# Attention over mirrored positions: context rows at p, 255-p, 256+p and 511-p, the reversed ones moved by index

## The chip, the cores and the metric

One Trainium2 chip, and of it one core. The metric is the time of one execution of the whole program on the device, in microseconds; lower is better. The program has five instruction streams of its own: TensorE (PE, with its weight loads apart as PEld), VectorE (DVE), ScalarE (ACT), GpSimd (POOL) and SyncE (SP). Each works through its instructions in the order written and waits for others by semaphores. SP and POOL also issue transfers between the memories. Those issued on POOL can add to what lies at their target (`accum_op`) and can take their row numbers from a tile (`indirect_dma_start`).

## The reference

`x` and `ctx` are 32 x 512 x 512 (batch, position, feature), float32. Two stages follow one another:

```python
q   = layernorm(x) * scale(norm of the row) * wave(position)
Q, K, V = q @ Wq.T + bq, (gain * ctx) @ Wk.T + bk, (gain * ctx) @ Wv.T + bv
Qf, Kf, Vf = (fft over the 512 positions)
QKV = hamilton(hamilton(Qf * filt, Kf * filt), Vf * filt)   # quaternion products in four blocks of 128 features
x   = x + ifft(QKV).real
t   = layernorm(layernorm(x)) * gamma + beta                # 16384 tokens
e   = argmax(t @ gate.T);  slot = rank among the tokens of expert e, kept while below 1024
x   = x + layernorm(x) + weight * (gelu(t @ wi[e]) @ wo[e]) # 8 experts, 512 -> 2048 -> 512
```

Since the inputs are real, half of the frequencies do. The transform is a matrix product with tables of cosines and sines.

## The kernel before

**Attention and routing** (`attention_and_routing`) runs over the 32 batch rows. For each row the 512 positions lie in four tiles of 128 (`TC = 4`). Position n and n+256 are folded: their sum gives the even frequencies, their difference the odd ones. The sum is folded once more for the even ones. `load` brings a row in on SP; `fold` (L422, L424) on DVE and `fold_sum` (L430, an accumulating transfer on POOL) fold both the context (`cs`) and the scaled input (`qs`). `forward` (L452, L457) then makes, for each of four chunks of 128 features, 256 odd columns out of two tiles of 128 positions and two times 128 even columns out of one tile each, all in one PSUM tile of the pool `ps_f` (two buffers); ACT copies it out (L465).

`project` (L483) multiplies frequencies by Wk, Wq and Wv, in two halves of frequencies (c = 0 even, 1 odd), each into one tile of `ps_p` (two buffers). ACT takes the upper half out (`halves`, L499), DVE makes the blocks from it (`block`, L506). For c = 0 the Nyquist frequency lies in a row of its own, which goes through memory and back (`nyquist_lanes`: L525 and L533 on SP, L538 and the spreads L545 to L547 on POOL). `matrix_product` (L586 to L599) makes the two quaternion products on DVE, `components` (L610 to L618) lays the result down as `y`.

The way back is in two parts. `inverse_even` (L646) has four matmuls that contract over 64 frequencies each; `second` (L652) and `even` (L656) combine them. `inverse_odd` (L661) has two matmuls for each of two position tiles, and `odd` (L672) adds and subtracts and sums at the same time. `means` (L683) makes the mean of it, and `add_input` (L701, POOL) adds the input `x` from memory, 1024 KB. One and two rows later come the second normalisation (`square` L695, `norms`, `token` L759, `result` L767 on ACT), two stores on SP (L772: the tokens to `tokbuf`, the result to `out`), the tokens' transposes (L781), the gate (`logits`, `shares`, `add_shares`), `choose`, `ranks` (L861, L862: rank by a triangular matrix) and `place`; `scatter` (L887, POOL) writes token number and weight of each token at its expert's slot into `meta`, four index transfers a row.

`stats` (L342, L346 on ACT) reads a second copy of `x` ahead of time for its mean and variance; `factors` makes the scale of several rows at once out of it with some 60 small DVE instructions, spread in steps.

**The order.** Everything in this stage is put on a written time line: `at(time, function)`, `steps(time, step, generator)`, with `ROW = 61.0` as the written length of a row. `plan.run()` issues in order of these times and `in_order` fixes that order on each engine. The written times order instructions; they hold nothing back on the chip.

**Experts** (`experts`): for each of 8 experts 2 x 512 slots are gathered from `tokbuf` by index (L1220), transposed (L1238) and sent through two matrix products (L1109), made of seven instead of eight block products (sums on DVE), and scaled and added to `out` by index (L1259). `ms` (L1197, SP) reads `meta` back once before.

Of the kernel before, what the change touches and what calls it, by code (L numbers as in the profile page):

```python
# [11 lines left out]
F32 = mybir.dt.float32  # L12
# [5 lines left out]
P = 128  # L18
# [11 lines left out]
def _constants():  # L30
# [11 lines left out]

    sig = lambda v: 1.0 / (1.0 + np.exp(-v))
# [8 lines left out]
    fwd, fwdq, inv = [], [], []  # L52
    for c in range(2):
# [3 lines left out]
        e = np.exp(-2j * np.pi / S * ((np.arange(h)[:, None] * k[None, :]) % S))  # L57
        herm = np.zeros(P, np.complex128)
# [6 lines left out]
        f, q, i = pack(e), pack(e * herm), pack(e)  # L65
        if c == 0:
            alt = 1.0 - 2.0 * (n % 2)
            f[:, P] = i[:, P] = alt
            q[:, P] = alt * filt3[h].real
        fwd.append(f)  # L70
        fwdq.append(q)
        inv.append(i.T * (0.5 * gain * gain / S))
    def parts(even, odd):
        even = even[0:P].reshape(P, 2, 2, P // 2).transpose(0, 2, 1, 3).reshape(P, 1, 2 * P)
        return np.concatenate([even, odd.reshape(2, P, 2 * P).transpose(1, 0, 2)], axis=1)

    fwd, fwdq = (parts(*a) for a in (fwd, fwdq))
    inv = [a.reshape(2, P, h).transpose(1, 0, 2) for a in inv]
    inv = np.concatenate([inv[0][:, :, 0:P], inv[1]], axis=2)
# [17 lines left out]
def tile_xattn_ffn(ctx: ExitStack, tc: tile.TileContext, a: dict, gain: float):  # L97
# [10 lines left out]
    meta = [dram.tile([n_slot, 2], I32, name=f"meta{t}") for t in range(TC)]  # L108
# [103 lines left out]
def attention_and_routing(tc, a, gain, ident, gamma, beta, tokbuf, meta):  # L212
    nc = tc.nc
    x_in, ctx_in = a["x"], a["ctx"]
    H = TC // 2
# [8 lines left out]
    ROW = 61.0  # L224
    base = [0.0] + [53.1 + ROW * b for b in range(B + 2)]
    end = base[B]
    marks = {}
    with ExitStack() as es:
# [25 lines left out]
        rows = lambda ap: ap.rearrange("(c p) n -> p c n", p=P)  # L254
        w = [{} for _ in range(B)]
# [4 lines left out]
        fwd = fwdp.tile([P, 1 + H, 2 * P], F32, name="fwd")  # L260
        fwdq = fwdp.tile([P, 1 + H, 2 * P], F32, name="fwdq")
        inv = wp.tile([P, 2, P + HS], F32, name="inv")
# [7 lines left out]
        tri = wp.tile([P, P], F32, name="tri")  # L270
        iota8 = wp.tile([P, TC, E], F32, name="iota8")
        iota8m = wp.tile([P, TC, E], F32, name="iota8m")
        itok = wp.tile([P, TC], F32, name="itok")
        empty = wp.tile([P, E * CAP // P, 2], I32, name="empty")
# [34 lines left out]
        def small_tables():  # L309
            nc.vector.memset(gate, 0.0)  # L310
            nc.vector.memset(ones, 1.0)
            nc.vector.memset(empty[:, :, 0], int(UNFILLED))
            nc.vector.memset(empty[:, :, 1], 0)

            nc.gpsimd.affine_select(
                tri, ones, pattern=[[1, P]], compare_op=ALU.is_gt, fill=0.0, base=0, channel_multiplier=-1
            )
            for t, pattern, by in ((iota8, [[0, TC], [1, E]], 0), (itok, [[P, TC]], 1)):
                nc.gpsimd.iota(
                    t, pattern=pattern, base=0, channel_multiplier=by, allow_small_or_imprecise_dtypes=True  # L320
                )
# [33 lines left out]
        def first_stats(t):  # L355

            if "mx" not in w[0]:
                w[0]["mx"] = sm.tile([P, TC, 2], F32, tag="mv", name="mx")
            mv = w[0]["mx"]
            st = sm.tile([P, 6], F32, tag="bnst", name=f"bx_{t}")  # L360
            nc.vector.bn_stats(st, w[0]["xs"][:, t, :])
            nc.vector.bn_aggr(mv[:, t, :], st)
            if t == TC - 1:
                nc.vector.tensor_scalar(nmean[:, 0, :], mv[:, :, 0], -1.0, None, ALU.mult)
                nc.vector.tensor_scalar(vsum[:, 0, :], mv[:, :, 1], float(D), None, ALU.mult)
# [45 lines left out]
        def load(b, n, src):  # L411
            w[b][n] = inp.tile([P, TC, D], F32, tag=n, name=f"{n}_{b}")
            nc.sync.dma_start(w[b][n], tok_rows(src[b]))

        def fold(b, n, tag, i):


            if i == 0:
                w[b][tag] = foldp.tile([P, 2, H, D], F32, tag=tag, name=f"{tag}_{b}")
            src, to = w[b][n], w[b][tag]  # L420
            if i == 0:
                tt(to[:, 1], src[:, 0:H, :], src[:, H:TC, :], ALU.subtract)  # L422
            else:
                tt(to[:, 0, i - 1, :], src[:, 0, :], src[:, 1, :], (ALU.add, ALU.subtract)[i - 1])  # L424

        def fold_sum(b, n):

            src = w[b][n]
            upper = src[:, H:TC, :] if n == "x" else tok_rows(ctx_in[b])[:, H:TC, :]
            nc.gpsimd.dma_start(src[:, 0:H, :], upper, accum_op=ALU.add)  # L430

        def fold_sum_now(b, n):
            src = w[b][n]
            tt(src[:, 0:H, :], src[:, 0:H, :], src[:, H:TC, :], ALU.add)
# [9 lines left out]
        def forward(b, src, table, tag, t):  # L444

            def mm(dc):
# [3 lines left out]
                even = ps[:, 0:HS].rearrange("p (r q f) -> p q r f", r=2, q=2)  # L450
                for i in range(H):
                    nc.tensor.matmul(  # L452
                        ps[:, HS:], w[b][src][:, 1, i, dc * P : (dc + 1) * P], table[:, 1 + i, :],
                        start=(i == 0), stop=(i == H - 1),
                    )
# [7 lines left out]
            for dc in range(DC):  # L463
                at(t + 1.31 * dc, mm, dc)
                at(t + 1.31 * (dc + 1) + 0.05, lambda dc=dc: nc.scalar.copy(w[b][tag][:, dc, :], w[b]["ps", tag, dc]))  # L465
# [880 lines left out]
```

## Time and profile before

| | |
|---|---|
| time, three runs | 3691.69 us median (3690.15 to 3692.68) |
| the profiled execution | 3692.56 us, its span 3690.9 us |
| mean granted TensorE clock | 0.986 |
| first matmul of row 0, of row 1, of row 31 | 10.44, 75.27, 1943.31 us |
| a plain row, from its first `ps_cf` matmul to the next row's | 61.32 us |
| first gather of the experts, first transposes of theirs | 2078.57, 2086.26 us |
| from the experts' first product to the end | 2094.01 to 3690.9 us |

A line of a group gives the source line, engine, operation, tiles and shapes, the number of instructions, their busy time, the mean time of one, and the idle time of the engine before them with what ended it. A line of the timeline gives start and length in us, and in brackets the idle time before it. `LDWEIGHTS` are weight loads, `DMA_DIRECT2D` and `DMA_INDIRECT` the issue of a transfer and not its movement. Names stand without buffer numbers.

### The profile page before, as it was taken

What the parts mean: (1) busy time and instruction counts of PE and PEld (TensorE: products, weight loads), DVE (VectorE), ACT (ScalarE), POOL (GpSimd) and SP (SyncE); (2) the same over time, 40 slices, a digit from 0 to 9 for tenths busy, and PEclk for the clock granted to TensorE, in tenths of its full rate; (3) what the DMA queues carried; (4) which work ended last, traced back from release to release, by engine and by line L of the source; (5) the groups of instructions that cost most, each with busy time, mean ns of one, the idle gap of its engine ahead of it and who ended that gap; (6) DMA issues with size and microseconds to landing.
All of it is one profiled execution on the core that took longest, in us unless ns stands there. A gap on an engine that the chain in (4) does not pass through costs nothing. (4 is left out here: it accounts for less than half of the span.)

```text
span 3690.9 us, 39046 instructions
## 1 busy us (share of the span) xinstructions
PE 3576.5 (97%) x14208; PEld 2461.0 (67%) x14208; DVE 2548.0 (69%) x4768; ACT 1342.5 (36%) x2563; POOL 626.9 (17%) x626
## 2 busy tenths in 40 slices
PE   8899999999999999999998599999999999999998
PEld 4455455545555545555554488888888888888887
DVE  7898989989898989898988444344444444443532
ACT  5556565645454434444443311211222222111211
POOL 2122122223231212121211111011111111111100
PEclk9999999999999999999999799999999999999999
DMA  5454455454544343434333402031313121121200
GB/s 182 126 137 130 134 138 137 132 132 110 131 112 107 94 101 101 109 99 110 98 83 95 125 23 89 12 100 35 103 35 92 46 66 54 46 69 41 86 1 1
DMA packets 256585, 334.06 MB, mean 91 GB/s; under 512 B 69572, under 2 KB 136132, under 8 KB 256391
## 3 DMA queue, kind: packets, MB, share of 16 engines
q1 hardware_dynamic: 205970, 239.92, 19.4%
q0 software_dynamic: 50128, 91.24, 14.0%
q8 instruction: 112, 1.84, 0.2%
q14 instruction: 81, 0.66, 0.1%
q10 hardware_dynamic: 294, 0.40, 0.0%
HBM read 239.63 MB, written 84.55 MB: 88 GB/s over the span
## 5 line engine op out<-in xcount | busy, mean ns | idle before, releaser
L1109 PE MATMUL r_o<-wo,h 128*128 128x256 f32 x3584 | 781.2, 379 | 0.0
L1109 PE MATMUL r<-xt,wi 128*128 128x256 f32 x3584 | 777.9, 379 | 0.8 <-DVE u L1124 0.8
L1109 PEld LDWEIGHTS r<-xt,wi 128*128 128x128 f32 x3584 | 681.7, 190 | 93.7 <-DVE u L1124 1.1
L1109 PEld LDWEIGHTS r_o<-wo,h 128*128 128x128 f32 x3584 | 677.5, 190 | 90.3
L483 PE MATMUL pp_v<-wv,cf 128*128 128x512 f32 x1024 | 459.5, 597 | 2.4 <-DVE u L396 2.3
L483 PE MATMUL pp_k<-wk,cf 128*128 128x512 f32 x1024 | 458.8, 596 | 0.0
L483 PE MATMUL pp_q<-wq,qf 128*128 128x512 f32 x1024 | 454.7, 592 | 0.0
L483 PEld LDWEIGHTS pp_k<-wk,cf 128*128 128x128 f32 x1024 | 190.1, 191 | 242.1 <-issue 236.3
L483 PEld LDWEIGHTS pp_q<-wq,qf 128*128 128x128 f32 x1024 | 192.2, 190 | 230.1 <-issue 223.6
L1285 ACT ACTIVATE h<-h 128x512 f32<-128x512 f32 x256 | 160.2, 631 | 472.3 <-DVE h L1117 471.2
L483 PEld LDWEIGHTS pp_v<-wv,cf 128*128 128x128 f32 x1024 | 188.1, 191 | 206.7 <-issue 203.5
L887 POOL DMA_INDIRECT meta<-row,slot x128 | 226.1, 1766 | 447.4 <-DVE slot L877 391.8
L1259 POOL DMA_INDIRECT out<-o,tid x64 | 107.1, 1674 | 916.0 <-ACT o L1256 802.5
L586 DVE TENSOR_TENSOR pa<-blk 128x1024 f32<-128x1024 f32 (+1 forms) x128 | 156.8, 1225 | 111.0 <-POOL blk L547 99.9
L1256 ACT ACTIVATE o<-u_o,wgt 128x256 f32<-128x256 f32 x96 | 43.7, 502 | 385.7 <-DVE u_o L1117 385.7
L1124 DVE TENSOR_TENSOR u_o<-r_o,p_o 128x512 f32<-128x512 f32 x16 | 11.1, 693 | 239.6 <-PE r_o L1109 239.6
L1117 DVE TENSOR_TENSOR h<-r,u 128x512 f32<-128x512 f32 x192 | 129.0, 687 | 68.7 <-PE r L1109 68.7
L1220 POOL DMA_INDIRECT g<-tokbuf,gid x64 | 79.5, 1242 | 514.5 <-PE ept L1238 490.8
L589 DVE TENSOR_TENSOR pa<-pa,pb 128x1024 f32<-128x1024 f32 (+1 forms) x128 | 157.1, 1227 | 2.0
L661 PE MATMUL odd<-y,inv 128*128 128x512 f32 x256 | 126.1, 629 | 31.9 <-DVE r L656 20.2
L586 DVE TENSOR_TENSOR pb<-blk 128x1024 f32<-128x1024 f32 (+1 forms) x128 | 156.7, 1224 | 0.0
L591 DVE TENSOR_TENSOR pa<-pa,pb 128x1024 f32<-128x1024 f32 (+1 forms) x128 | 156.4, 1222 | 0.0
(197 smaller groups left out, 4813.9 us busy)
## 6 DMA issues: line engine op xcount, KB each, us to landing
ctx<-in_ctx SPq DMA_DIRECT2D x32, 1024.0 KB
xs<-in_x SPq DMA_DIRECT2D x32, 1024.0 KB
x<-in_x SPq DMA_DIRECT2D x32, 1024.0 KB
r<-in_x POOLq DMA_DIRECT2D x32, 1024.0 KB
tokbuf<-tok SPq DMA_DIRECT2D x32, 1024.0 KB
out<-r SPq DMA_DIRECT2D x32, 1024.0 KB
wi<-in_wi SPq DMA_DIRECT2D x64, 512.0 KB
wo<-in_wo SPq DMA_DIRECT2D x32, 1024.0 KB
```

The source lines that it names most:

```text
L483: nc.tensor.matmul(w[b][key][:, ri, :], w[b][f][:, dc, lo : lo + P], wt[n][:, dc, :], start=(dc == 0), stop=(dc == DC - 1),)
L586: tt(out, _bc(left, full), right, ALU.mult)
L589: tt(pa[:, :, 0], pa[:, :, 0], pb[:, :, 1], ALU.subtract)
L591: tt(pa[:, :, 1], pa[:, :, 1], pb[:, :, 0], ALU.add)
L661: nc.tensor.matmul(ps, inv[:, ri, (1 + t) * P : (2 + t) * P], w[b]["y"][:, 1, ri, :], start=(ri == 0), stop=(ri == 1))
L887: nc.gpsimd.indirect_dma_start(out=meta[t], out_offset=bass.IndirectOffsetOnAxis(ap=w[b]["slot"][:, t : t + 1], axis=0), in_=w[b]["row"][: ...
L1109: nc.tensor.matmul(to[:, m, :], lhs(a, m, i), rhs(b, i), start=(i == 0), stop=(i == k - 1))
L1117: tt(c[i], x, y, ALU.add)
L1220: nc.gpsimd.indirect_dma_start(out=t, out_offset=None, in_=tokbuf, in_offset=bass.IndirectOffsetOnAxis(ap=gid[:, e, c : c + 1], axis=0), b ...
L1256: nc.scalar.activation(o[:, d * N : (d + 1) * N], c[2 * h + d][:, m, :], AF.Copy, scale=wgt[:, e, col : col + 1])
L1259: nc.gpsimd.indirect_dma_start(out=a["out"], out_offset=bass.IndirectOffsetOnAxis(ap=tid[:, e, col : col + 1], axis=0), in_=o, in_offset=None,
L1285: [lambda o=o: nc.scalar.activation(o, o, AF.Gelu) for o in out],
```

## The change

The context's positions are laid down in four mirrored places: partition p holds p, 255-p, 256+p and 511-p. The two forward places come with one plain load (`onward`), the two reversed ones by index transfers of 128 rows each (`behind`, with the row numbers in `back`). Sums and differences over these four places separate cosines from sines as well as even from odd frequencies. So the context's forward transform has four matmuls of 128 columns for each chunk, and the odd frequencies need one tile of places where they had two. The way back is four matmuls of 512 columns over 128 frequencies, cosines and sines apart, in the order (even, odd); `sines`, `part`, `upper` and `lower` put the four places together. The input path keeps its positions and its table.

With it move: the context's sums and half of the input's go to accumulating transfers on POOL (`add_ctx`, `add_x`, `add_x_quarters`, `lower`), negated copies to ACT (`minus_ctx`, `minus_x`, `signed_x`), the sums for the mean to ACT (`sum_up`), which now runs after the input is added. Input and result meet the mirrored layout by index: `add_input` and the store to `out` are one plain and two index transfers each. `meta` has three words an entry, `ranks` two triangular matrices, and the written times are new, with `ROW = 57.5`, other times for nearly every step, and other groups of rows for `factors`. The core of it:

```diff
@@ attention_and_routing
-    ROW = 61.0
-    base = [0.0] + [53.1 + ROW * b for b in range(B + 2)]
+    ROW = 57.5
+    base = [0.0] + [50.4 + ROW * b for b in range(B + 2)]
+        def onward(ap):
+            return ap.rearrange("(h w p) d -> w p h d", h=H, p=P)[0]
+
+        def behind(b, ap, tiles, store=False, add=False):
+            for h, t in enumerate(tiles):
+                at_row = bass.IndirectOffsetOnAxis(ap=back[:, b, h : h + 1], axis=0)
+                ins = nc.gpsimd.indirect_dma_start(
+                    out=ap if store else t,
+                    out_offset=at_row if store else None,
+                    in_=t if store else ap,
+                    in_offset=None if store else at_row,
+                    bounds_check=n_tok - 1,
+                    oob_is_err=False,
+                    **({"compute_op": ALU.add} if add else {}),
+                )
+            return ins
...
-                tt(to[:, 1], src[:, 0:H, :], src[:, H:TC, :], ALU.subtract)
-                tt(to[:, 0, i - 1, :], src[:, 0, :], src[:, 1, :], (ALU.add, ALU.subtract)[i - 1])
-            nc.gpsimd.dma_start(src[:, 0:H, :], upper, accum_op=ALU.add)
...
+        def load_ctx(b):
+            w[b]["ctx"] = c = inp.tile([P, 2, H, D], F32, tag="ctx", name=f"ctx_{b}")
+            nc.sync.dma_start(c[:, 0], onward(ctx_in[b]))
+            behind(b, flat_rows(ctx_in), [c[:, 1, h] for h in range(H)])
+        def minus_ctx(b):
+            c = w[b]["ctx"][:, 1]
+            nc.scalar.activation(c, c, AF.Copy, scale=-1.0)
+        def add_ctx(b, i):
+            c = w[b]["ctx"]
+            nc.gpsimd.dma_start(c[:, i], onward(ctx_in[b]) if i else c[:, 1], accum_op=ALU.add)
+        def fold_ctx(b, i):
...
+            tt(w[b]["cs"][:, i], c[:, :, 0], c[:, :, 1], (ALU.add, ALU.subtract)[i])
+        def minus_x(b):
+            new_qs(b)
+            nc.scalar.activation(w[b]["qs"][:, 1], w[b]["x"][:, H:TC, :], AF.Copy, scale=-1.0)
+        def add_x(b, i):
+            to = w[b]["x"][:, H:TC, :] if i else w[b]["qs"][:, 1]
+            nc.gpsimd.dma_start(to, w[b]["x"][:, 0:H, :], accum_op=ALU.add)
+        def signed_x(b, i):
+            nc.scalar.activation(w[b]["qs"][:, 0, i, :], w[b]["x"][:, 3, :], AF.Copy, scale=(1.0, -1.0)[i])
+        def add_x_quarters(b):
+            nc.gpsimd.dma_start(
+                w[b]["qs"][:, 0], w[b]["x"][:, 2:3, :].to_broadcast([P, H, D]), accum_op=ALU.add
+            )
...
+            def context(ps, dc):
+                for i, to in ((0, 0), (2, 3), (1, 1), (3, 2)):
+                    nc.tensor.matmul(
+                        ps[:, to * P : (to + 1) * P], w[b]["cs"][:, i // 2, i % 2, dc * P : (dc + 1) * P], fwd[:, i, :],
+                        start=True, stop=True,
+                    )
...
+        def inverse(b, c):
+            for ri in range(2):
+                w[b]["ps", c, ri] = ps = ps_f.tile([P, D], F32, tag="psf", name=f"back_{b}_{c}_{ri}")
+                nc.tensor.matmul(ps, inv[:, 2 * c + ri, :], w[b]["y"][:, c, ri, :], start=True, stop=True)
+        def sines(b, c):
...
+            nc.scalar.copy(si, w[b]["ps", c, 1])
+        def part(b, c, i):
+            co, si = w[b]["ps", c, 0], w[b]["si", c]
+            if c == 0:
+                tt(w[b]["r"][:, i, :], co, si, (ALU.add, ALU.subtract)[i])
+            else:
+                w[b]["odd"] = w[b]["y"][:, 0]
+                tt(w[b]["odd"][:, i, :], *((si, co) if i else (co, si)), (ALU.add, ALU.subtract)[i])
+        def upper(b):
+            tt(w[b]["r"][:, H:TC, :], w[b]["r"][:, 0:H, :], w[b]["odd"], ALU.subtract)
+        def lower(b, now=False):
...
+                nc.gpsimd.dma_start(r, w[b]["odd"], accum_op=ALU.add)
+        def add_input(b, way):
+            r = w[b]["r"]
+            if way:
+                behind(b, flat_rows(x_in), [r[:, 2 * h + 1] for h in range(H)], add=True)
+            else:
+                nc.gpsimd.dma_start(r[:, 0::2, :], onward(x_in[b]), accum_op=ALU.add)
+        def sum_up(b, t):
+            r = w[b]["r"][:, t, :]
+            nc.scalar.activation(r, r, AF.Identity, accum_out=sums(b)[:, t : t + 1])
...
         def store(b, to, n):
-            marks[n, b] = nc.sync.dma_start(tok_rows(to[b * S : (b + 1) * S, :]), w[b][n])
+            rows = to[b * S : (b + 1) * S, :]
+            if n == "tok":
+                marks[n, b] = nc.sync.dma_start(tok_rows(rows), w[b][n])
+            else:
+                nc.sync.dma_start(onward(rows), w[b][n][:, 0::2, :])
+                marks[n, b] = behind(b, to, [w[b][n][:, 2 * h + 1] for h in range(H)], store=True)
...
-            nc.tensor.matmul(flat(rk), tri, flat(w[b]["hot"]), start=True, stop=False)
-            nc.tensor.matmul(flat(rk), ones, flat(before[b][:, 0:TC, :]), start=False, stop=True)
+            for way in range(2):
+                to = rk[:, way::2, :]
+                nc.tensor.matmul(to, tri[way], w[b]["hot"][:, way::2, :], start=True, stop=False)
+                nc.tensor.matmul(to, ones, before[b][:, way:TC:2, :], start=False, stop=True)
...
             forward(b, "cf", o, 0.875)
```

## The prediction

> **What bounds the kernel now.** I read the page first, then the stretches of equal rows, TensorE's timeline over one row, and the waits. (A row is one of the 32 batch rows; between two rows' first ps_cf matmuls.)
>
> ```profile
> PE 3576.5 (97%) x14208; PEld 2461.0 (67%) x14208; DVE 2548.0 (69%) x4768; ACT 1342.5 (36%) x2563; POOL 626.9 (17%) x626
> 895.25:956.57 61.32, 61.32 (x213) 33.19 (x212) 55.24 (x105) 32.18 (x64) 16.21 (x16) 1.00 0.47 121
> 1636.72:1698.04 61.32, 61.32 (x214) 33.20 (x213) 55.38 (x105) 26.90 (x47) 11.91 (x16) 1.00 0.42 104
> 1326.68:1391.01 64.33, 61.59 (x214) 33.11 (x213) 58.25 (x134) 26.81 (x47) 12.21 (x16) 1.00 0.39 99
> PE odd L661 <- DVE r L656: 20.2, 10, 6.9
> DVE pa L586 <- POOL blk L547: 99.9, 28, 5.4
> ```
>
> The first line is the page's busy time of each engine. The stretches give length, then busy time of PE, PEld, DVE, ACT and POOL with instruction counts, then granted clock, DMA share and GB/s; the last two lines are waits: who waited for whom, us in total, times, longest. A plain row takes 61.32 us and PE fills all of it, at full clock: PE sets the row. DVE has only 6 us to spare. In 1326.68:1391.01 the code adds 29 small DVE instructions (`factors`), DVE grows by 2.9 us and the row by 3.0: PE then waits for `even` (L656) to free a PSUM tile. This is the only PE wait of weight between rows 1 and 31.
>
> ```profile
> 1201.85 1.03 PE L452 MATMUL ps_cf<-fwd,cs 128*128 128x256 f32 x4
> 1202.71 0.61 PE L457 MATMUL ps_cf<-fwd,cs 128*128 128x128 f32 x4
> 1203.15 1.03 PE L452 MATMUL ps_cf<-fwd,cs 128*128 128x256 f32 x4
> 1222.62 0.60 PE L781 MATMUL pt<-ident,tok 128*128 128x128 f32 x4
> 1223.06 3.60 PE L483 MATMUL pp_q<-wq,qf 128*128 128x512 f32 x8
> 1234.77 1.99 PE L646 MATMUL even<-y,inv 64*128 64x512 f32 x8
> 1236.69 1.06 PE L798 MATMUL lp<-tokT,gate 128*32 128x512 f32 x8
> 1242.03 4.02 PE L661 MATMUL odd<-y,inv 128*128 128x512 f32 x8
> 1245.89 3.60 PE L483 MATMUL pp_k<-wk,cf 128*128 128x512 f32 x8
> ```
>
> Distances of starts are the real prices (ends overlap): one context chunk 1.31 us, of which four 128-column records take 0.44; four 128x128 transposes 0.44, so 0.11 a record; eight 512-column records 3.44; the even way back 1.92, the odd 3.86.
>
> **PE, part by part.** (1) Context forward: four chunks of sixteen records that were half 256 wide become four of eight records, 128 wide: 8 x 0.11 = 0.875 us each. Saved 4 x (1.31 - 0.875) = 1.74 us. (A matmul leaves two records here: four of 256 columns are two matmuls.) (2) Way back: 1.92 + 3.86 = 5.78 becomes four full matmuls, 3.44. Saved 2.34. The Trainium skill, "TensorEngine Tiling (Array Packing)", section "When to Use Tiling", speaks against giving up the even half: contracting over 64 rows allows two row tiles at once, which would be worth a factor of two. By it the old even part should take 1.72 and odd 3.44, and the saving is 5.16 - 3.44 = 1.72. The trace has 1.92 and 3.86 (0.42 of the latter waits for L656), so I take 2.34. (3) `ranks`: four small matmuls for two; L861 and L862 took 0.36 together, so +0.34. Net 3.74: row 57.6. A context chunk now fills a PSUM tile every 0.875 us, with two tiles; ACT's copy takes 0.59 (L465) and begins some 0.2 after the matmul, so a tile comes free 1.67 after its chunk's start, needed at 1.75. For this I add 0.15 (0 to 0.8). Row 57.75, 3.57 less; over rows 1 to 31 110.7 us, and 1.7 in row 0: 112.4.
>
> **DVE and its waits.** Removed per row at the timeline's cadence: L422 and L424 for both inputs 4.7, L656 1.3, L672 2.7, L683 and L847 0.2. Added: two 1024-wide context folds 2.3, four `part` 2.7 (L656's price), `upper` 1.1. Net -2.8: 52.6 of 57.75, a margin as thin as before. But both ways back now free their PSUM before the next row's forward, and `factors` is spread over more rows. From 75.27 to 1943.31 the rows lost 1868.0 - 30 x 61.32 = 28.4 us; I expect 17 back (6 of the rest in rows 1 to 3, 5 in rows 4 to 15; bounds 0 and 28). With L656's stall gone, what is late next is `block` (L506): it frees the projections' two PSUM tiles. q0's must be free before k1 starts, 8 us after DVE's turn by the written times, so DVE may lag by several us before PE stops.
>
> **ACT.** Added: `minus_ctx`, `minus_x` (1024 wide; no such row: between 0.96, twice the 0.48 cadence of a 512-wide copy, and 1.6, twice L439's 0.81; I take 1.1 each), `signed_x` 1.0, `sum_up` 2.5 (L342's cadence), one more copy 0.5, `means` 0.2; a gain is excluded, it is all new work. 26.9 + 6.4 = 33.3, and 5.3 (32.2 - 26.9) for each row's statistics, two in rows 1 to 14: 43.9 of 57.75. PE covers it; if that cover goes, it is the PSUM copies that come late.
>
> **POOL and DMA.** Here nearly all new work lies. Per row six index transfers (two each for the context load, the input added, the result's store), five direct transfers in place of three, and all in one queue with `offset`, the spreads and the four scatters.
>
> ```profile
> 832.68 5.89 POOL L887 DMA_INDIRECT meta<-row,slot  x1 [12.69 <-DVE slot L877]
> 838.87 2.01 POOL L887 DMA_INDIRECT meta<-row,slot  x1 [0.30 <-issue]
> 1261.77 1.28 POOL L887 DMA_INDIRECT meta<-row,slot  x1 [12.22 <-DVE slot L877]
> 1263.36 1.43 POOL L887 DMA_INDIRECT meta<-row,slot  x1 [0.30 <-issue]
>   POOL out L1259: 105.3, 37
> ```
>
> Ten index transfers at L887's mean 1.77 + 0.30 are 20.7; `add_x` twice, `add_ctx` twice, the quarters, `lower`, half of the input at 0.93 to 1.36 (L430, L701) 7.3; `blk<-bias` 1.7; spreads 1.9: 31.6. Waits: the input waits for `lower` to land (an L430 transfer landed within 7.4 us, issue 1222.29 to its reader at 1229.69), the first store for SP's half of the same store (5), the second for the first, since both write `out` (105.3 / 37 = 2.85). Behind these stand the scatters and the second `add_ctx`, for which `fold_ctx` on DVE waits. Sum 47, 10 below the row: no PE time. By the page "SBUF — State Buffer", section "Who interferes with whom", a DVE instruction with two SBUF inputs contends with a GpSimd one that reads SBUF, and one blocks the other fully. Then the six would each wait out a run of L586 and L589, as the 5.89 seems to: 6 x 4.6 = 28 more, a round of 75, over the row. But at 1261.77 the issue lay under four L586 in a row and took 1.28. I take the row's mean. SP issues as many transfers as before, context and result half as large, so its queue costs nothing more. DMA share: about 2.1 MB more are accumulated per row (four of 512 KB). The page's q0 moved 91.24 MB in 14.0% of the span, 5.7 us a MB: 12 us more on the 25.7 of a plain row (0.42 x 61.3), 0.65 of 57.75, and 0.7 with statistics: busy, not full; a transfer that must land within 8 us of its issue still does.
>
> **Start and tail.** The first context rows come by index after an iota: PE starts 1 to 3 us later, and row 0 waits less for statistics (DVE waited 8.6 for ACT there). The other moves of row 0 (weight v turned on ACT, row 1's statistics on DVE) go with these: zero, between -4 and +4. In the tail row 30's two indexed stores stand on POOL ahead of row 31's scatters, and wait for SP's half. That was issued at 2061.58, the scatters began at 2063.45. Now 0.4 + 5 + 1.6 + 2.85 + 1.6 come first: scatters near 2073, and the first gather (2078.57) 9.5 late. SP's `ms` loads (12 bytes an entry for 8) are behind row 31's store as well, but the `wo` load, which was issued just ahead of them at 2065.29, now stands earlier: -2.5, for `ms` took 7 us from its issue at 2069.76 to its reader at 2076.82. Net +7, between 0 and 15.
>
> **Sum.** Against the profiled execution's own 3692.56 (span 3690.9 and 1.7 around it): 3692.56 - 112.4 - 17 + 7 = 3570.2. It lies 0.9 above the median shown, so 3569. The experts, 1597 us from 2094 on, keep their code.
>
> **Rivals.** A: ACT late in rows 1 to 14. 43.9 busy in strict order, with waits for landings (`sum_up`) among the PSUM copies. For: the density. Against: ACT was at 36 to 39 of 61 in such rows before with hardly a PE wait. If they run at 59.8: 14 x 2 = 28, so 3597. B: 128-wide matmuls limited by their weight load: a LDWEIGHTS lasts 190 ns. If each record took that, the context costs 6.1, not 3.5: 32 x 2.6 = 83, so 3652. Against: the transposes' 0.11. C: POOL's round partly blocked. With 5.89 for the first of two series and waits of 19 in place of 15: 31.6 + 9.2 + 19 = 60, rows of 60: 30 x 2.25 = 67, so 3636. D, slower: the same queue, its place the store pair. If under a DMA share of 0.65 every landing waited for (`lower`, SP's half, the first store) takes the 7 us that L430's took at most, and three series begin with a 5.89, a round is 31.6 + 21 + 3 x 4.6 = 66. The change loses from a round of about 61.6 on; at 66 it is 30 x (66 - 57.75) = 248 on 3569, so 3817. For: each POOL wait holds all that is behind it. Against: 10 us of room by the mean. E: nothing moves, since PE waits for DVE as before (61.3 rows).
>
> **Chances.** Forecast 0.60 (its own range 3540 to 3590), A 0.13, B 0.04, C 0.10, D 0.11, E 0.02. Faster 0.87, same 0.02, slower 0.11; 0.2%, 7 us, is what a measurement of this kernel can tell from no change. Low end: all 28 us of waits gone, rows at 57.6, tail 0: 3540. High: takes in A, B and half of C: 3650.
>
> **What would show it.** Right: rows of 57.6 to 58.2 between first ps_cf matmuls with PE full, chunks 0.875 apart, four back matmuls in 3.44, POOL near 30 busy a row, first gather later after row 31 than 135 us. Wrong: a PE wait named ACT cf/qf or DVE blk in plain rows; DVE `cs` waiting for a DMA in every row; POOL without idle time.

## The result and the profile after

The changed kernel takes 3643.94 us (median of 4 runs, 3643.74 to 3645.2) beside 3691.44 before: ratio 0.9872, interval 0.9855 to 0.9889. It is faster, by 47.5 us, where the prediction had 122. The first matmuls of the rows cut the profiled executions into three pieces:

| us | before | after | moved | predicted |
|---|---|---|---|---|
| start to row 1's first matmul | 75.27 | 67.31 | -7.96 | -1.7 |
| rows 1 to 30 | 1868.04 | 1828.85 | -39.2 | -124.1 |
| row 31's first matmul to the end | 1747.6 | 1745.9 | -1.7 | +3.4 |
| span | 3690.9 | 3642.1 | -48.8 | -122.4 |

The last column is the prediction's sum by the same pieces: 3.57 on TensorE for each row, 17 of waits, +7 in the tail. Start and tail came out a few microseconds better; all that is missing, 85 us, is missing in rows 1 to 30. From the page, the stretches of two rows (length, then busy PE, PEld, DVE, ACT, POOL, granted clock, DMA share, GB/s), and the waits of PE and DVE:

```profile
PE 3486.9 (96%) x14080; PEld 2414.2 (66%) x14080; DVE 2467.8 (68%) x4494; ACT 1524.3 (42%) x2981; POOL 1024.4 (28%) x946
1657.00:1716.77 59.77, 58.75 (x209) 31.67 (x208) 52.51 (x94) 32.98 (x61) 28.36 (x25) 1.00 0.63 142
867.84:929.14 61.30, 58.74 (x209) 31.68 (x208) 54.19 (x111) 38.28 (x78) 27.78 (x27) 1.00 0.64 146
PE pp_v L573 <- DVE before L947: 24.6, 20, 2.2
PE pp_v L573 <- DVE blk L596: 18.6, 21, 3.6
DVE pa L676 <- DMA blk<-bias: 136.9, 44, 5.4
DVE pa L676 <- POOL blk L637: 53.9, 17, 5.4
```

A plain row fell from 61.32 to between 59.4 and 60.5. DVE, ACT, POOL and the DMA share are busy much as forecast (52.6, 33.3, 31.6 and 0.65). New are the two waits of PE in the list: PE, which waited for nothing in a plain row before, now waits for DVE to free `ps_p`. The prediction had named a wait for `blk` in plain rows as a sign of being wrong. And DVE, with 52.5 us of work in a row of 59.8, itself waits, above all for `blk<-bias`: the `offset` transfer, which adds the bias to one row of `blk` ahead of each quaternion product for c = 0. Where that wait arises is read from the timelines of POOL and DVE over one row (start, length, in brackets the idle time before):

```profile
1692.84 1.22 POOL L512 DMA_DIRECT2D qs<-x  x1 [1.85 <-ACT qs L508]
1695.27 0.90 POOL L759 DMA_DIRECT2D r<-y  x1 [1.21 <-DVE den L967]
1700.52 0.81 POOL L628 DMA_DIRECT2D blk<-bias  x1 [4.35 <-DVE slot L982]
1702.08 0.69 DVE L689 TENSOR_TENSOR o<-pa 128x516 f32<-128x516 f32 x1
1706.81 1.23 DVE L676 TENSOR_TENSOR pa<-o,blk 128x1032 f32<-128x1032 f32 x1 [4.04 <-DMA blk<-bias]
```

In before, the same pair stood so:

```profile
1241.85 0.83 POOL L538 DMA_DIRECT2D blk<-bias  x1 [7.34 <-DVE blk L506]
1242.60 1.41 DVE L656 TENSOR_TENSOR r<-even,r 128x512 f32<-128x512 f32 x2
1245.14 0.68 DVE L672 SCALAR_TENSOR_TENSOR r<-r,odd 128x512 f32<-128x512 f32 x1
1248.81 1.23 DVE L586 TENSOR_TENSOR pa<-o,blk 128x1032 f32<-128x1032 f32 x1
```

Before, the second product began 6.96 us after the offset's issue, and DVE filled the time with the way back (L656, L672) and `choose`. After, that work is elsewhere: DVE is ready 2.3 us after the issue and starts 6.3 us after it, once the 4 KB have landed. Ahead of them in POOL's queue stand two new accumulating transfers of 512 KB, the quarters (`add_x_quarters`, L512) and `lower` (L759). On SP's queue two transfers were issued shortly before, `load_x` (L446, 1024 KB) and the plain half of a store to `out`:

```profile
1698.38 1.60 SPq L446 DMA_DIRECT2D x<-in_x  x1
1700.09 0.50 SPq L875 DMA_DIRECT2D out<-r  x1
```

### The profile page after: what moved, and what is told of

Its sections match the earlier page's. It is cut to its first block, busy times and chain, and to the rows that moved or that the text cites. A ratio compares the mean times of both kernels' runs of the same rounds, so it can differ in the third digit from the quotient of the medians.

```text
span 3642.1 us, 39892 instructions
## 1 busy us (share of the span) xinstructions
PE 3486.9 (96%) x14080; PEld 2414.2 (66%) x14080; DVE 2467.8 (68%) x4494; ACT 1524.3 (42%) x2981; POOL 1024.4 (28%) x946
## 3 DMA queue, kind: packets, MB, share of 16 engines
q0 software_dynamic: 83088, 189.84, 26.1%
q1 hardware_dynamic: 189586, 206.50, 18.1%
## 5 line engine op out<-in xcount | busy, mean ns | idle before, releaser
L573 PE MATMUL pp_v<-wv,cf 128*128 128x512 f32 x1024 | 470.0, 603 | 56.5 <-DVE before L947 24.6
L1385 POOL DMA_INDIRECT out<-o,ids x64 | 106.8, 1668 | 912.5 <-ACT o L1382 803.1
L1346 POOL DMA_INDIRECT g<-tokbuf,ids x64 | 80.4, 1256 | 508.9 <-PE ept L1364 490.5
L676 DVE TENSOR_TENSOR pa<-o,blk 128x1032 f32<-128x1032 f32 (+1 forms) x124 | 152.1, 1227 | 103.8 <-DMA blk<-bias 60.5
L676 DVE TENSOR_TENSOR pa<-blk 128x1024 f32<-128x1024 f32 (+1 forms) x128 | 156.3, 1221 | 87.1 <-DMA blk<-bias 75.5
L1382 ACT ACTIVATE o<-u_o,wgt 128x256 f32<-128x256 f32 x96 | 43.5, 500 | 385.8 <-DVE u_o L1241 385.8
L992 POOL DMA_INDIRECT meta<-entry,slot x128 | 167.3, 1307 | 57.1 <-issue 36.9
L896 ACT ACTIVATE tokT<-pt,beta,gamma 128x512 f32<-128x512 f32 x124 | 96.1, 777 | 177.2 <-PE pt L885 168.7
L271 POOL DMA_INDIRECT out<-r,back x64 | 124.8, 1950 | 126.6 <-ACT cf L555 50.9
L679 DVE TENSOR_TENSOR pa<-pa,pb 128x1024 f32<-128x1024 f32 (+1 forms) x128 | 157.1, 1227 | 2.9
```

Source lines behind the costliest of these rows:

```text
L271: ins = nc.gpsimd.indirect_dma_start(out=ap if store else t, out_offset=at_row if store else None, in_=t if store else ap, in_offset=None ...
L573: nc.tensor.matmul(w[b][key][:, ri, :], w[b][f][:, dc, lo : lo + P], wt[n][:, dc, :], start=(dc == 0), stop=(dc == DC - 1),)
L676: tt(out, _bc(left, full), right, ALU.mult)
L679: tt(pa[:, :, 0], pa[:, :, 0], pb[:, :, 1], ALU.subtract)
L896: nc.scalar.activation(to, ps, AF.Identity, bias=o, scale=g)
L992: nc.gpsimd.indirect_dma_start(out=meta[t], out_offset=bass.IndirectOffsetOnAxis(ap=w[b]["slot"][:, t : t + 1], axis=0), in_=entry[:, b, t ...
```

## The experiments

Theory 1: the transfers ahead of the offset in POOL's queue make it land late, DVE has nothing left to cover that, and PE waits for DVE. Rivals: it is the offset's own latency; POOL's round with its index transfers; ACT; or the load on the DMA engines, from whichever queue. All edits are against the changed kernel. "Rows" is the sum of rows 1 to 30, and 30 rows at TensorE's own pace, shown below to be 58.27, would be 1748.1. "Waits" is DVE's for `blk<-bias` in the whole run.

| kernel | median us | ratio to before | rows | waits (times) |
|---|---|---|---|---|
| the changed kernel | 3643.94 | 0.9872 [0.9855, 0.9889] | 1828.9 | 136.9 (44) |
| e1_no_bias | 3606.95 | 0.9772 [0.9756, 0.9788] | 1788.9 | none |
| e2_ring_order | 3649.82 | 0.9888 [0.9872, 0.9905] | 1832.9 | 66.5 (20) |
| e3_way_back_between | 3615.41 | 0.9791 [0.9774, 0.9807] | 1805.3 | 44.1 (12) |
| e4_lower_on_dve | 3601.93 | 0.9761 [0.9744, 0.9777] | 1782.0 | 10.1 (6) |
| e5_lower_alone | 3624.66 | 0.9810 [0.9793, 0.9826] | 1805.1 | 68.6 (30) |
| e6_quarters_alone | 3592.53 | 0.9724 [0.9707, 0.9740] | 1774.8 | 13.7 (9) |
| e7_floor | 3596.33 | 0.9732 [0.9716, 0.9748] | 1781.5 | none |
| e8_plain_not_indexed | 3625.18 | 0.9808 [0.9792, 0.9825] | 1820.4 | 103.2 (33) |
| e9_half_quarters | 3631.43 | 0.9823 [0.9808, 0.9839] | 1808.4 | 99.5 (33) |
| e10_same_bytes_other_queue | 3599.26 | 0.9736 [0.9721, 0.9751] | 1784.7 | 14.4 (8) |
| e11_quarters_and_tail | 3600.11 | 0.9743 [0.9729, 0.9756] | 1779.0 | 18.2 (8) |
| e12_row29_store_first | 3584.17 | 0.9705 [0.9688, 0.9721] | 1779.5 | 21.6 (11) |

**The offset taken away (e1).**

```diff
 def nyquist_lanes(b, lo, hi, t, t_blk):
-            at(t_blk, offset)
```

> Leaves out the accumulating transfer of the biases (offset, L628), so bq, bk and bv are missing from the result; nothing else is changed. Theory 1: DVE sets the row of the changed kernel (52.5 us of work and 6 to 7 of waits), and most of the waits are for the landing of blk<-bias (136.9 us in 44 waits). Without it the rows go from about 60.3 to about 58.8, where TensorE alone sets them: 1.5 x 30 = 45 us, so about 3599. Theory 2: the waits only fill time that DVE would lose elsewhere, behind the spreads of the Nyquist lanes (L637): rows stay at 60 and the time within 8 us of 3644.

37 us less. Most rows from 16 on are 58.27 or 58.28 long. PE is then busy throughout, so this is TensorE's own length of a row:

```profile
1740.91:1799.18 58.27, 58.27 (x209) 31.83 (x208) 52.69 (x95) 32.96 (x61) 23.53 (x24) 1.00 0.67 145
```

About half of what rows 1 to 30 hold over TensorE's pace (80.7 us) goes with the offset, nearly all of it in the later rows: rows 14 to 30 fall from 1028.3 to 993.7 us, rows 3 to 13 only from 667.1 to 666.8. In those DVE waits for the spread (L637) instead, as the run's theory 2 had it: 127.6 us in the whole run, 53.9 before. The spread needs `nyi`, which comes back over SP's queue:

```profile
671.48 0.18 POOL L635 COPY blk<-nyi 128x4 f32<-128x4 f32 x1 [11.80 <-DMA nyi<-nyid]
```

Whether the offset is late by its own latency or by other transfers, this run can't say.

**Order in the queue, first attempt (e2).** The quarters and `lower` both go behind the second offset, and `load_x`, which overwrites what the quarters read, later with them:

```diff
-            at(t1 + 4.6, lower, b)
+            at(t1 + (11.0 if 0 < b < B - 2 else 4.6), lower, b)
-                    at(o + tf + 1.3, add_x_quarters, b + 1)
+                    at(o + (39.1 if 1 < b < B - 1 else tf + 1.3), add_x_quarters, b + 1)
-                at(o + tl, load_x, b + 2)
+                at(o + (46.0 if b > 1 else tl), load_x, b + 2)
```

> Only the order on POOL changes in rows 2 to 29: add_x_quarters and lower (512 KB each) are issued after the second offset and its spread instead of before; load_x stands 5.5 us later on SP. Theory 1 with the ring as the cause: the 4 KB of the second bias wait behind 1.5 MB of accumulating transfers; issued ahead of two thirds of them they land in about 2 us as before instead of 6.3, DVE's second wait (about 4 us a row) falls to 0 or 1, rows at about 59: 28 x 1.3 = 36 us, so about 3608. Theory 1 with a fixed latency of such a transfer as the cause (nothing between the two products for DVE to do): no change within 8 us. Theory 2: no change.

No gain, and yet the second offset was cured. POOL's and DVE's timelines:

```profile
1700.90 0.81 POOL L628 DMA_DIRECT2D blk<-bias  x1 [11.55 <-DVE slot L982]
1703.26 1.23 DVE L676 TENSOR_TENSOR pa<-o,blk 128x1032 f32<-128x1032 f32 x1
1703.39 2.02 POOL L759 DMA_DIRECT2D r<-y  x1
1711.60 1.21 POOL L766 DMA_DIRECT2D r<-in_x  x1 [6.19 <-DMA r<-y]
1678.03 1.22 DVE L480 TENSOR_TENSOR cs<-ctx 128x1024 f32<-128x1024 f32 x1 [3.83 <-issue]
```

The offset is used 2.4 us after its issue, with no wait shown. But the input may only be added once `lower` has landed, and `lower` now comes just ahead of it: POOL stands still for 6.2 us, 173.5 in 27 rows, and all behind it in the queue comes later by as much. `add_ctx` is among it, and `fold_ctx` (L480) on DVE has 82.5 us of idle time before it in 25 places, where the changed kernel has none of weight. One wait had been traded for another. This is the prediction's own warning ("each POOL wait holds all that is behind it"), met in an experiment instead of the change.

**Something put between the products again (e3).** The quarters as in e2, `lower` as in the change, and the odd way back set between the two products:

```diff
-                residual(b, o1 + 22.6, o1 + 28.2, o1 + 41.0)
+                residual(b, o1 + 22.6, o1 + (36.5 if 0 < b < B - 2 else 28.2), o1 + (43.0 if 0 < b < B - 2 else 41.0))
```

> Rows 2 to 29: the odd way back (inverse, sines, part, upper, lower) is written 8.3 us later, so that DVE has 2.5 us of it to do between the first and the second product, and lower and add_x_quarters stand behind the second offset on POOL; add_input 2 us later. Theory 1: the wait for the second bias goes altogether, rows at 58.8: 28 x 1.5 = 42 us, about 3602. Against it: lower lands later, the input after it, and ACT's sum_up stands among the PSUM copies of the next row: then a new wait DMA at L775 and the row is not shorter, 3644 or more. Theory 2: no change.

28 us less, short of the 42 expected. `lower` follows the odd way back and so again stands just before the input, with a wait like e2's on POOL.

**`lower` on DVE, and the quarters moved (e4).**

```diff
-            at(t1 + 4.6, lower, b)
+            at(t1 + 4.6, lower, b, True)
```

> lower is done by DVE (1024 wide, 1.14 us) instead of by an accumulating transfer, in rows 0 to 30; add_x_quarters stands behind the second offset in rows 2 to 29. Theory 1 (ring): the second bias has neither before it: its landing falls from 6.3 us to 2 or 3, for 1.14 us more of DVE work; DVE 53.6 + 3 of waits, below TensorE's 58.8, so rows near 59: about 3606. If DVE's own work is the bound and not its waits, rows get 1.1 us longer: 3677. Theory 2: no change or up to 30 us slower.

42 us less, near the expectation; but the edit has two parts. They were then tried one by one.

**The two parts (e5: `lower` on DVE alone; e6: the quarters and `load_x` alone, as in e2, `lower` as in the change).**

> After the change, with one edit: lower is an addition on DVE (1.2 us a row more there), for which one accumulating transfer of 512 KB a row is gone from POOL's queue; the quarters stay where they were. Theory 1 (the second offset lands late because accumulating transfers issued shortly before it lie ahead in the same queue): only the quarters are left ahead, issued 7.7 us before the offset instead of 5.2 (lower), so most of the wait of 4 us at the second product goes: plain rows of 58.3 to 59, about 3605. Rival (in the kernel with both edits the gain came from moving the quarters; lower itself counts little): about 3640.

> After the change, with the quarters put behind the second offset and the spread, and load_x later; lower stays an accumulating transfer, ahead of the second offset by 5 us. Theory 1: one transfer of 512 KB less ahead of the offset, it lands some 2 us sooner, rows of 59 to 59.5, about 3620; nothing waits on POOL for lower's landing, since it lies long before the input is added, unlike the kernel in which lower was put behind the offset. Rival (lower alone is what is in the way): about 3640.

Both expectations were off, in opposite ways. `lower` alone gives 19 us and leaves 30 waits. The quarters and `load_x` give 51 us, more than e4, in which DVE has `lower` to do as well, 1.2 us a row. e6, the stretch of a row, POOL, DVE and SP's `load_x` in it, and the issues' list (size, median us from issue to landing):

```profile
1667.69:1725.97 58.28, 58.28 (x209) 31.85 (x208) 52.07 (x94) 32.97 (x61) 24.69 (x26) 1.00 0.64 141
1706.07 0.85 POOL L759 DMA_DIRECT2D r<-y  x1 [4.08 <-DVE den L967]
1711.31 0.81 POOL L628 DMA_DIRECT2D blk<-bias  x1 [4.39 <-DVE slot L982]
1713.01 1.89 POOL L512 DMA_DIRECT2D qs<-x  x1
1713.68 1.23 DVE L676 TENSOR_TENSOR pa<-o,blk 128x1032 f32<-128x1032 f32 x1
1718.82 0.37 SPq L446 DMA_DIRECT2D x<-in_x  x1
blk<-bias POOLq DMA_DIRECT2D x32, 4.0 KB, 2.2
```

From row 15 on nearly every row is TensorE's 58.27 again, with the same transfers and the same bytes as in the changed kernel. The places of two differ, the quarters and `load_x`. `lower`, 5.2 us ahead of the offset, does no harm.

Which of the two it is, e5 helps to tell. There the quarters are issued 10.4 us ahead of the offset (1668.76 and 1679.19), and DVE still waits for it. But the quarters land 5.1 us after their issue. From 1674.0 to the offset's issue POOL's queue (q0) moves nothing at all; SP's (q1) has `load_x` under way, and from 1679.2 to 1681.6 it holds the engines alone:

```profile
DMA to landing us min/median/max: 5.1/5.1/5.1
1674.30 1.18 SPq L446 DMA_DIRECT2D x<-in_x  x1
q1 hardware_dynamic: 469, 0.92, 103.0%
q0 software_dynamic: 3, 0.00, 0.5%
1682.49 1.24 DVE L676 TENSOR_TENSOR pa<-o,blk 128x1032 f32<-128x1032 f32 x1 [1.04 <-DMA blk<-bias]
```

So in this row nothing in its own queue held the offset back. The paragraph behind e10 takes this up for all rows.

**What is left of the offset (e7).** e4 without the offset.

> The kernel with lower on DVE and the quarters behind the second offset, and in addition the biases left out (no offset at all). It measures what is left of the offset once the transfers ahead of it are gone. Theory 1: nothing of weight waits on PE any more, rows from 3 on at TensorE's own 58.27, so 3597 less 27 x 0.7 = 19: about 3580. Rival (the offset still costs its landing): the rows shorten only where DVE waits for it now, 10 us in 6 rows, so 3590 to 3597.

3596.33 beside 3601.93; the ratios' intervals overlap. With the quarters, `lower` and `load_x` out of its way, the offset costs nothing that can be told: rows 1 to 30 take 1782.0 with it and 1781.5 without. The rows did not all fall to 58.27 (most 58.6 to 59.9), as theory 1 had expected: with `lower` on DVE, PE waits in 20 places for `blk` there (14.5 us in sum). The rival's numbers were the nearer.

**Index transfers made plain (e8).**

```diff
-                at_row = bass.IndirectOffsetOnAxis(ap=back[:, b, h : h + 1], axis=0)
-                ins = nc.gpsimd.indirect_dma_start(...)
+                plain = ap[b * S + h * HS + P : b * S + h * HS + 2 * P, :]
+                ins = nc.gpsimd.dma_start(plain if store else t, t if store else plain, **({"accum_op": ALU.add} if add else {}))
```

> After the change, with all six index transfers of a row (context load, input added, result stored) replaced by plain ones of the same bytes on the same queue, so these positions are not reversed (another computation, same amount of work). It prices the index transfers' issue on POOL. Theory 1 (landings in the queue matter, not POOL's issue time): POOL less busy by some us a row and the time within 10 us of the changed kernel, 3635 to 3650. Rival C (POOL's round is what delays): rows shorter by 1 us and more, below 3615.

19 us less, between the two expectations. POOL's work in a plain row falls from 24 to 28 us to about 21, but rows 1 to 30 lose only 8.5 us, 0.3 a row: rival C, POOL's issue, is not what holds the rows. Ten of the 19 come after row 31's first matmul. The first gather came 138.3 us after it in the changed kernel and 128.6 here. That is taken up in e11 and e12.

**Half the bytes (e9).** The quarters at their old place, one half of them:

```diff
-                w[b]["qs"][:, 0], w[b]["x"][:, 2:3, :].to_broadcast([P, H, D]), accum_op=ALU.add
+                w[b]["qs"][:, 0, 0:1, :], w[b]["x"][:, 2:3, :], accum_op=ALU.add
```

> The changed kernel with the quarters at their old place, but only the first of their two halves moved (256 KB in place of 512; the other half of the addition is left out). Theory 1 (the second offset waits for the bytes ahead of it in its queue): its landing, 5.7 us on average where DVE waits for it, falls by about half of what moving the quarters away saved, rows of 59.3, about 3618, between the changed kernel's 3644 and the 3592 with the quarters out of the way. Rival (each transfer ahead costs a fixed time, whatever its size): 3640. Rival (any cut below a threshold frees it): 3595.

Between the ends, as theory 1 said, though nearer the changed kernel: a third of the way in the ratio (0.9872, 0.9823, 0.9724), DVE's waits down from 136.9 to 99.5 us. The size counts, and is not all: `load_x` keeps its place here.

**The same bytes on the other queue (e10).** e6 with a copy of 512 KB between two places of memory on SP at the quarters' former written time.

```diff
+                if 1 < b < B - 1:
+                    at(o + tf + 1.3, spare, b)   # nc.sync.dma_start(room, x_in[b, 0 : S // 2, :])
```

> The kernel with the quarters behind the second offset, and in addition a plain copy of 512 KB between two places of memory, issued on SP where the quarters had stood. It tells order in POOL's queue from load on the shared DMA engines. Theory 1 (order in the queue): the offset does not stand behind it, time within 8 us of the 3592 without the copy. Rival (bytes in flight on the engines, whatever the queue): the offset lands as late as in the changed kernel, rows of 60, 3630 to 3645.

No difference from e6 in the whole time that can be told. But as a test of the load on the engines it fails in the later rows: in the row looked at, the copy was issued at 1651.75 and the offset at 1663.61, 11.9 us later, where the quarters had stood 7.7 ahead and `load_x` 2.1.

**Early and late rows in these traces.** Up to row 13 each row also loads `x` twice for the statistics (`xs`, 1024 KB each). Sums of the rows' lengths, from one trace of each kernel:

| us | rows 3 to 13 | rows 14 to 30 |
|---|---|---|
| at TensorE's pace | 641.0 | 990.6 |
| the changed kernel | 667.1 | 1028.3 |
| e1_no_bias | 666.8 | 993.7 |
| e5_lower_alone | 652.4 | 1020.3 |
| e6_quarters_alone | 649.0 | 994.2 |
| e9_half_quarters | 659.0 | 1016.0 |
| e10_same_bytes_other_queue | 659.4 | 994.9 |

In the row of the changed kernel shown further up, SP's queue (q1) and POOL's (q0) moved this from 1701.5 to 1705.5, while the offset was under way (packets, MB, share of the 16 engines):

```profile
q1 hardware_dynamic: 659, 1.28, 95.6%
q0 software_dynamic: 16, 0.00, 0.4%
```

- **Rows 14 to 30** have 110.7 of the 136.9 us of waits for the offset. In rows 14 to 29 of the changed kernel the last of its packets begins 4.2 to 5.7 us after its issue, and SP's queue, with `load_x` and the store to `out`, takes 0.8 to 1.0 of the engines in that time (0.5 in row 21). In the same rows of e6, with `load_x` behind the offset, SP moves nothing and the packet begins after 1.6 to 1.8 us. In e5, with POOL's own queue empty for 3.7 to 6.1 us before the issue and SP's not, it begins after 1.9 to 4.5. So in these rows the late landing goes with SP's load and not with what stands ahead in POOL's queue: the queue in theory 1 is the wrong one for them, and the rival, load on the engines from whichever queue, fits. No run moved `load_x` alone, so this is read from the traces and not shown by an experiment.
- **Rows 3 to 13** gain nothing from leaving the offset out, and much from taking 512 KB out of this stretch: 14.7 us with `lower` on DVE, 18.1 with the quarters and `load_x` later, 8.1 with half of the quarters gone. The copy of 512 KB on SP (e10) makes them 659.4 long, where the three kernels with e6's order and no copy have 649.0 to 654.1 (e6, e11, e12). Here POOL's queue is still moving its large transfers when the offset is issued; but bytes on SP's queue cost as well, and what DVE waits for most is the spread (45.2 us; 16.0 for the offset), whose `nyi` comes over SP.

**The tail (e11, e12).** First the prediction's reading of it: row 30's indexed stores hold row 31's scatters back. e11 puts them behind the scatters, on top of e6:

```diff
+                at(end + 43.4, store_behind, b, a["out"], "r")   # left out of store for b == B - 2
-        with after(marks["r", B - 2]):
+        with after(marks["tok", B - 2]):
```

> Best version so far (quarters behind the second offset) with one more edit: in the tail the two indexed stores of row 30 stand on POOL behind row 31's scatters instead of ahead of them, and the load of wo follows row 30's tokens. Theory (those stores hold the scatters back by some 10 us, as the kernel with plain transfers showed: first gather 128.6 us after row 31's first matmul, 138.3 in the changed kernel): scatters some 10 us sooner, the first gather 4 to 8 us sooner because the four stores now stand ahead of it alone; 3585 to 3589. Rival (the gathers wait for the same stores anyway): 3592.

Nothing gained, 8 lost by the medians. Counted from row 31's first matmul, the scatters start at 122.6 us, hardly sooner than the 124.0 of e6: the slots are not ready before. SP then stood before `ms` with row 31's store behind it, so that the gathers came at 147.3 instead of 138.8. The prediction's reading was wrong. What the tail waits for stands in ACT's waits, in the changed kernel and in e8:

```profile
ACT r L739 <- DMA out<-r,back: 15.8, 1, 15.8
ACT r L733 <- PE back L726: 4.3, 1, 4.3
```

The first copy of row 31's way back writes the buffer from which row 29's second indexed store still reads, and those two stores stood behind four scatters, 11.5 us apart (1953.70 and 1965.23). e12 puts row 29's store ahead of those scatters, on top of e6:

```diff
-                at(o2 + 48.5, store, b, a["out"], "r")
+                at(o2 + (44.9 if b == B - 3 else 48.5), store, b, a["out"], "r")
```

> Best version so far (quarters behind the second offset), with the store of row 29's result put ahead of row 30's predecessor's four scatters on POOL, nothing else. It tests where the tail's price lies: in the changed kernel ACT waits 16.0 us at its first copy of the last row's way back, named as waiting for out<-r,back, the second indexed store of row 29, whose buffer that copy writes; with plain stores it waits 4.3. Theory (this store holds back row 31): the pair is issued some 6 us sooner, ACT's wait falls from 16.0 to about 10, and the first gather comes 5 to 6 us sooner than 138.8 after row 31's first matmul. Rival (another thing holds it, the store is only the last to be named): the first gather stays at 138 to 139. The whole time, 3592 before, should go to about 3587, which the measurement can hardly tell apart; the trace decides.

```profile
ACT r L739 <- PE back L732: 4.0, 1, 4.0
1975.88 1.05 POOL L1346 DMA_INDIRECT g<-tokbuf,ids  x1 [3.79 <-DVE ids L1339]
```

ACT's wait for the store is gone, and the first gather comes 129.0 us after row 31's first matmul (1846.84) where e6 had 138.8. 3584.17 us, ratio 0.9705 [0.9688, 0.9721]: the lowest of all, 109 us below the 3693.24 of before beside it, and it differs from the changed kernel in three written times only.

## Why the prediction was right in its sign and wrong in its size

- **The step that failed** is the sentence under POOL and DMA that a transfer which must land within 8 us of its issue still does, taken from a mean DMA share of 0.65, and with it `blk<-bias` priced at 1.7 us of issue alone. The share came out as forecast (0.63), and yet SP's queue alone took 95.6% of the engines while the offset was under way. The 8 us were before's deadline: there too the last packet began up to 4.5 us after the issue in some rows, and DVE, busy with the way back, came 7 us after it. The change took L656 and L672 out of that gap, so that DVE is there after 2.3 us. And it brought `load_x` closer, to 2.0 to 5.0 us ahead of the offset in rows 14 to 29 (9.3 to 10.0 in before).
- **What that step cost**: DVE waits 136.9 us for the offset and, with 52.5 us of work and some 6 of waits in a row, sets the row at 59.4 to 60.5. Leaving the offset out gives back 34.6 of the 37.7 us that rows 14 to 30 hold over TensorE's pace, moving the quarters and `load_x` 34.1. The 26.1 us of rows 3 to 13 do not hang on the offset (0.3); there e6 gives 18.1 back. That the offset's landing costs the 34 us is shown by e1; that `load_x` is what delays it is read from the traces.
- **TensorE's own row** was mis-sized too: 58.27 instead of 57.75, 15.6 us over 30 rows. The terms: context forward 5.24 to 3.62, 1.62 saved instead of 1.74; `ranks` 0.37 to 0.81; the way back 5.42 to 3.52, 1.90 saved instead of 2.34. For the last one the odd part was taken at 3.86 from a row in which it waited for L656, as the prediction noted beside it. A row without that wait has 3.51:

```profile
1615.59 3.68 PE L661 MATMUL odd<-y,inv 128*128 128x512 f32 x8
1619.10 3.60 PE L483 MATMUL pp_k<-wk,cf 128*128 128x512 f32 x8
1681.72 1.88 PE L732 MATMUL back<-y,inv 128*128 128x512 f32 x4
1657.00 3.78 PE L528 MATMUL ps_cf<-fwd,cs 128*128 128x128 f32 x32
1660.62 1.08 PE L536 MATMUL ps_qf<-fwdq,qs 128*128 128x256 f32 x4
```

- The Trainium skill's rule for contracting over 64 rows ("TensorEngine Tiling (Array Packing)", "When to Use Tiling") puts the saving, as the prediction's estimate from it, at 1.72. The measured 1.90 lies nearer to it than the 2.34: the even part had run at 1.91 for what full matmuls would do in 3.44.
- **The recovery of 17 us of waits** did not come: the rows hold 80.7 us over 58.27 each, instead of 11. Of this, rows 1 and 2 alone are 16.9 (68.89 and 64.56 long, granted clock 0.90 and 0.95), and they stay so in e6 and e12. They were much the same before (69.28 and 65.78). Their cause was not tried: it is open.
- **Start**: the first matmul came 2.7 us later, as predicted (1 to 3), but row 0 took 54.2 instead of 64.8, so that the start gained 8 where zero was put down beside the forward's 1.7.
- **Tail**: +7 beside row 31's own -3.6 was predicted, -1.7 came. The first gather is 3 us later after row 31's first matmul, but not behind row 30's stores: it is row 29's store and its buffer (e12).
- **Index transfers**: POOL's 23 to 28 us of work a row stayed under the 31.6. e6 keeps all six index transfers and its rows come down to TensorE's 58.27, and plain ones in their place (e8) shorten a row of the changed kernel by 0.3 us, so the rounds of the rivals C and D did not set it. As the prediction read the Trainium skill's rule on shared access ("SBUF — State Buffer", "Who interferes with whom"), every issue would have waited out a run of products. Some do, 5.81 us at 1658.88 beside four L676; the mean of `out<-r,back` is 1.95.
- **ACT** (rival A) was busy as forecast, 33.0 us in plain rows and 43.5 with two rows' statistics, and PE hardly waited for it. **B** did not happen: 32 records of 128 columns took 3.62 us. **D**'s principle, a POOL wait that holds back all behind it, is what spoiled e2.

## What to carry to other kernels

A mean DMA share over a row says nothing of the few microseconds in which a small transfer has to land. For every transfer that an engine waits for, note when it is issued, when its reader arrives, and which large transfers, on any queue, are under way then. When a change takes work out of a gap, ask what landed under that work; the deadline read from the old trace moves with it. Before moving a large transfer behind a small one, look at who waits for the large one: e2 and e6 differ in one written time, and by 57 us in the medians. And where one edit has to move two transfers, as e6 does, its gain names neither of them: look in the traces what was moving when the small one was late.

## What the runs showed of the hardware

- A wait of TensorE can cost more than its length. In the row of the changed kernel from 321.05, PE waited 2.2 us in one piece, the granted clock was 0.97 and PE was busy for 60.5 us instead of some 58.7. The clock stood at 0.50 from 350.55 to 353.9, just after that wait, and at 1.00 in the rest of the row. Over rows 3 to 30 of all the traces, the longest wait of PE in a row was 1.94 us or more in 23 rows. In 13 of them the clock was 0.97 or 0.95 (longest waits of 1.94 to 4.17 us), in ten it was 1.00 (1.96 to 2.88); all rows with shorter waits kept 1.00. What decides between the two, and that the wait brings the clock down, was not tested. The last line below is e11's.

```profile
321.05:384.08 63.03, 60.49 (x209) 32.27 (x208) 55.20 (x122) 43.53 (x95) 25.65 (x27) 0.97 0.72 176
PE pp_v L573 <- DVE before L947: 2.2, 1, 2.2
350.55:353.90 3.35, 3.35 (x6) 1.27 (x5) 3.20 (x11) 3.35 (x7) 1.28 (x4) 0.50 0.54 186
729.51:794.71 65.20, 61.02 (x210) 32.70 (x209) 56.47 (x115) 43.64 (x95) 27.04 (x28) 0.95 0.80 176
```

- A transfer of 4 KB on POOL's queue began its last packet 1.6 to 1.8 us after its issue with hardly anything else under way (e6, rows 14 to 29), and 1.9 to 4.5 us after it while SP's queue was moving a load of 1024 KB, though POOL's own queue had been empty for 3.7 to 6.1 us before (e5, same rows).
